# A fused attention and recurrence kernel: position biases from row and column sums on GpSimd, raw last chunks, another order at the end and a branch hint

## The chip, the cores and the metric

The kernel runs on one core of one Trainium2 chip. The metric is the device time of one execution in microseconds. Names of engines: PE is TensorE, DVE is VectorE, ACT is ScalarE, POOL is GpSimd, SP is SyncE; PEld is TensorE's weight load.

## What is computed

The input x has the shape (8, 128, 48, 48): 8 images, 128 channels, 2304 positions. Cut to what matters:

```python
# layer 0: causal attention on the group-normed image, with a position table (32 rows) appended
x0 = concat([gn(x), pe], axis=1).reshape(B, 160, N)
q, k, v = (leaky_relu(W @ x0 + b) for W, b in ((Wq, bq), (Wk, bk), (Wv, bv)))
x = x + softmax(mask(q.T @ k / sqrt(128))) @ v
# layer 1: attention of the normed tokens with themselves, then a recurrence over the positions
t = tokens(x)
n = ln(t);  t2 = t + softmax(n @ n.T) @ n
wx = ln(t2) @ W.T;  wx = (wx - mean(wx)) * rsqrt(var(wx) + 1e-5) * gamma + beta     # over all tokens
y_p = sigmoid(wx_p + y_{p-1} @ V.T)          # p = 0 .. 2303, y_{-1} = 0
out = t2 + y
```

The position table has two halves: row j < 16 depends only on the image row, row j >= 16 only on the image column. A last row of ones carries the biases. So the part of q and k that comes from the table is, for each channel, a value of the image row plus a value of the image column.

## The kernel before

`fast_path` computes everything under two assumptions (bounded logits; a recurrence that forgets its start), tests them at the end, writes `flag`, and `conv_attn_hybrid_kernel` (L1703) branches on it: at a flag of zero it jumps over `general_path`, a long program that does the work again without the assumptions.

**The attention part.** Each image's 2304 positions are cut into six chunks of 384 (`QC`), each of three blocks of 128. For image b the class `Causal` runs the first attention: for chunk j and block m a product `s` (L1038), its exponential `p` on ScalarE (L1040), on the diagonal a multiplication with a triangle on GpSimd (L1043), and a product `o` (L1049). The sums of p go to VectorE (`acc`, L1060, L1064). `Full` does the second attention in the same way (L1316, L1318, L1341), but uses each p twice: a transposed copy goes to memory (`e`) and comes back as `g` for another chunk (L1329). The tiles p come from six buffers, and products `o` follow their `s` three items later (`LAG`).

The order of instructions on each engine is written out by the program itself: `Stream` keeps chains of small steps with the costs that their author gave them, and runs a step when its time has come; a step with an empty engine name is a pure delay. `st.advance` and `st.finish` force steps of a chain to be emitted now. What the hardware then does is in order on each engine; DMAs are issued by SyncE in the order of its queue, a few by GpSimd.

**The head.** For image 0, `positions(n, j)` (L836 to L853) multiplies the position table's 33 rows with the weights of q, k (j = 0, 1: one product of 384 columns, L847) and v (j = 2: three of 128, L850), and ScalarE copies the result from PSUM into a tile `pb` (L851), which is also stored for the other images (L853). Beside it VectorE computes the group norm: six `bn_stats` (L805) as pieces of x land (`load_x`, three pieces of two chunks), an aggregate, two small products, and a power on GpSimd (L669). `project` (from L875) then norms a chunk (`xn`, L892), multiplies it with the weights (L899, L902), adds `pb` (L906), applies the leaky ReLU (L907), and takes maxima for the bound on the logits (L921).

**After a chunk of the second attention.** `Full.after` copies o out of PSUM (L1361), transposes it (L957), computes t2, its mean and variance (L1376 to L1385, L938 to L941), and the root on GpSimd (`rooted`, L1398). For most chunks t2 is then turned by a store and a load (`spread` L1412, `fetch` L1416), multiplied raw with the centred weights (`product` L1424) and only then scaled by the root, which is spread over the partitions by memory (L1409, L1418). The mean falls out because the weights are centred. The last two chunks of the last image avoid memory: t2 is transposed (`keep_last`, `turned_back`, L965), and beside it a normed copy is made (`normed`, L952), transposed (`back`), and multiplied (`statistics`, L1464), with `bn_stats` on the result (L1469). `keep` (L1438 to L1445) collects t2 in a tile `t2c` for two chunks, of which there is one buffer; `store` writes it out. Ahead of it, `keep` forces the chunk before to be finished. `idle` (L1505) issues products of the identity with itself, which fill TensorE's waits.

**The recurrence.** The 2304 positions are cut into 96 segments of 24 in three groups, which run side by side from 10 warm-up steps ahead. Before it, the statistics of all chunks are joined (L1595), and scale and shift of the batch norm are computed. VectorE writes the scaled inputs into PSUM (`inputs`, L1617, L1620), TensorE adds the product with the state (L1666), ScalarE takes the sigmoid (L1667). t2 is added by GpSimd or VectorE and stored (`add_residual`, L1643 to L1647). A product with the bounds of the logits (`pw`, L1650) goes with `fl`. After the last step VectorE adds the last residuals, compares the states at the seams of the segments (`seams`, L1635 to L1638), and TensorE adds up the result for `flag` (L1695 to L1698).

## Time and profile before

| what | us |
|---|---|
| median of three runs | 1719.08 |
| the runs | 1713.53, 1719.08, 1719.97 |
| the profiled execution | 1715.02 |
| its span | 1713.3 |
| TensorE busy | 1687.8 |
| VectorE busy | 1209.1 |
| ScalarE busy | 684.8 |
| GpSimd busy | 449.9 |
| last sigmoid ends | 1698.06 |
| `flag` written | 1704.88 |

The page of the profile gives the busy time of each engine, a view of the span in 40 slices, the chain of work that ended last, and the costliest groups of instructions. A line such as "PE MATMUL o<-p,vT 128*128 128x384" is an instruction with its program line, the tile it writes, the tiles it reads, and its size. A product of float32 values is recorded as two instructions. "idle before <-releaser" is how long the engine stood still, and what ended that. Times in a timeline count from the start of the span.

### The profile page before, as it was taken

How to read it: one execution, taken by the hardware profiler on the slowest of the kernel's cores; microseconds unless marked ns; L12 is line 12 of the kernel's file. 1: busy time of each engine (PE TensorE's matmuls, PEld its weight loads, DVE VectorE, ACT ScalarE, POOL GpSimd, SP SyncE). 2: the span in 40 equal slices, each digit the busy share in tenths (PEclk: the TensorE clock that was granted, in tenths of full speed). 3: DMA queues.
4: the chain of work that ended last, by engine and by line, in shares of the span. 5: the costliest groups of instructions: out<-in, count | busy, mean ns of one | idle time of the engine just before them, and what ended most of it. 6: DMA issues, size and time to landing. Idle time of an engine off the chain costs nothing.

```text
span 1713.3 us, 22451 instructions
## 1 busy us (share of the span) xinstructions
PE 1687.8 (99%) x6259; PEld 1085.4 (63%) x6259; DVE 1209.1 (71%) x3297; ACT 684.8 (40%) x1300; POOL 449.9 (26%) x637
## 2 busy tenths in 40 slices
PE   9999999999999999999999999999999999999986
PEld 5666666666666666666666666666666666666665
DVE  5875578666886578865787568865798657974467
ACT  3344334433344324443244333443244442443355
POOL 1233122312133122322124112331213221341205
PEclk9999999999999999999999999999999999999998
DMA  3337763568445774368735684448743686347857
GB/s 122 101 89 210 225 200 109 131 193 251 129 129 145 238 230 128 79 189 244 205 101 130 199 252 139 125 130 244 227 146 71 176 244 207 81 96 211 237 221 223
DMA packets 316731, 291.67 MB, mean 170 GB/s; under 512 B 195793, under 2 KB 280690, under 8 KB 315956
## 3 DMA queue, kind: packets, MB, share of 16 engines
q1 hardware_dynamic: 306572, 268.76, 54.7%
q0 software_dynamic: 9792, 20.99, 4.5%
q8 instruction: 52, 0.85, 0.2%
q14 instruction: 83, 0.68, 0.1%
q10 hardware_dynamic: 232, 0.40, 0.1%
HBM read 164.13 MB, written 125.90 MB: 169 GB/s over the span
## 4 chain that ended last, share of the span: by engine, by line
PE 96%; DMA 2%; DVE 1%; SPq 0%; issue 0%; ACT 0%; DVEq 0%; ACTq 0%
PE s L1038 17%; PE s L1316 17%; PE o L1049 17%; PE o L1341 17%; PE o L1329 13%; PE pj L899 3%; PE pj L902 2%; PE o L1337 2%; PE z L1666 2%; PE wx L1424 2%; DMA g<-e 1%; PE of_t L957 1%; PE pb L847 0%; PE idle_last L1505 0%; DMA x<-in_x_dram 0%; DMA e<-t 0%
## 5 line engine op out<-in xcount | busy, mean ns | idle before, releaser
L1318 ACT ACTIVATE p<-s,shift 128x384 f32<-128x384 f32 (+2 forms) x504 | 274.2, 550 | 535.9 <-PE s L1316 436.8
L1040 ACT ACTIVATE p<-s 128x384 f32<-128x384 f32 (+2 forms) x504 | 229.4, 460 | 400.1 <-PE s L1038 323.6
L1038 PE MATMUL s<-q,k 128*128 128x384 f32 (+2 forms) x1008 | 380.6, 459 | 0.1
L1316 PE MATMUL s<-xh 128*128 128x384 f32 (+2 forms) x1008 | 379.2, 458 | 0.0
L1049 PE MATMUL o<-p,vT 128*128 128x384 f32 (+2 forms) x1008 | 377.5, 456 | 0.0
L1341 PE MATMUL o<-p,xhT 128*128 128x384 f32 (+2 forms) x1008 | 369.1, 456 | 0.0
L1281 DVE STREAM_TRANSPOSE t<-p 128x384 f32<-128x384 f32 x360 | 186.0, 553 | 170.8 <-DMA e<-t 106.3
L1329 PE MATMUL o<-g,xhT 128*128 128x384 f32 x720 | 282.2, 489 | 0.7 <-DMA g<-e 0.7
L1341 PEld LDWEIGHTS o<-p,xhT 128*128 128x128 f32 x1008 | 189.7, 190 | 120.3
L1049 PEld LDWEIGHTS o<-p,vT 128*128 128x128 f32 x1008 | 186.9, 190 | 109.9 <-POOL p L1043 2.0
L1316 PEld LDWEIGHTS s<-xh 128*128 128x128 f32 x1008 | 183.2, 191 | 99.6 <-issue 0.2
L1038 PEld LDWEIGHTS s<-q,k 128*128 128x128 f32 x1008 | 183.4, 190 | 99.0 <-issue 2.2
L1064 DVE TENSOR_TENSOR acc<-acc,p 128x384 f32<-128x384 f32 (+2 forms) x408 | 212.5, 521 | 23.1 <-DVE acc L1064 1.0
L1329 PEld LDWEIGHTS o<-g,xhT 128*128 128x128 f32 x720 | 132.6, 191 | 80.2 <-DMA g<-e 2.2
L1043 POOL TENSOR_TENSOR p<-p,triu 128x128 f32<-128x128 f32 x144 | 71.3, 497 | 356.1 <-ACT p L1040 355.8
L1266 POOL DMA_DIRECT2D gm<-m x192 | 105.3, 555 | 179.1 <-PE s L1316 63.2
L1262 POOL DMA_DIRECT2D m<-tm x48 | 29.9, 623 | 374.5 <-DVE tm L1249 374.5
L1138 POOL TENSOR_SCALAR xhT<-xhT 128x384 f32<-128x384 f32 x48 | 60.5, 1260 | 150.5 <-DVE yt L1150 121.2
L1249 DVE STREAM_TRANSPOSE tm<-p 128x256 f32<-128x256 f32 x96 | 33.9, 366 | 73.1 <-ACT p L1318 72.3
L899 PE MATMUL pj<-xn,wT 128*128 128x384 f32 x192 | 77.9, 488 | 1.5 <-DVE xn L892 1.5
L947 POOL TENSOR_TENSOR rs_c<-ve_c,mhalf 128x3 f32<-128x3 f32 x48 | 48.2, 1004 | 96.1 <-DVE ve_c L941 86.8
L906 DVE TENSOR_TENSOR q<-pj,pb 128x384 f32<-128x384 f32 x48 | 26.6, 554 | 50.1 <-PE pj L899 50.1
(256 smaller groups left out, 1681.1 us busy)
## 6 DMA issues: line engine op xcount, KB each, us to landing
e<-t SPq DMA_DIRECT2D x480, 144.0 KB
g<-e SPq DMA_DIRECT2D x120, 576.0 KB
pb<-posb_d SPq DMA_DIRECT2D x42, 576.0 KB
t1t<-in_x_tok_dram SPq DMA_DIRECT2D x48, 192.0 KB
m<-tm POOLq DMA_DIRECT2D x48, 192.0 KB, 4.3
gm<-m POOLq DMA_DIRECT2D x192, 48.0 KB, 3.8
t_d<-tt SPq DMA_DIRECT2D x184, 48.0 KB
t2x<-t_d SPq DMA_DIRECT2D x46, 192.0 KB
```

The lines of the kernel that those rows point to most:

```text
L899: nc.tensor.matmul(ps[:, :QC], wT[:, j, :], xn, start=True, stop=True)
L1038: nc.tensor.matmul(s[:, off:QC], keys[b][:, ts(m, P)], queries[b, j][:, off:], start=True, stop=True)
L1040: nc.scalar.activation(p[:, off:], s[:, off:QC], AF.Exp, scale=SCALE)
L1043: nc.gpsimd.tensor_mul(p[:, off : off + P], p[:, off : off + P], triu)
L1049: nc.tensor.matmul(o[:, off:QC], vals[b][:, ts(m, P)], p[:, off:], start=first, stop=last)
L1064: nc.vector.tensor_add(a[:, off:], a[:, off:], p[:, off:])
L1266: nc.gpsimd.dma_start(gm[ts(r, SQ)].rearrange("c a q r -> c a (q r)"), d.rearrange("(a c) b f -> b c a f", a=R)[r])
L1281: nc.vector.transpose(t[:, :, :, g, :].rearrange("p b j r -> p j b r"), p.rearrange("p (j b r) -> p j b r", j=QB, b=R))
L1316: nc.tensor.matmul(s[:, off:QC], xh[:, ts(m, P)], xh[:, j * QC + off : (j + 1) * QC], start=True, stop=True)
L1318: nc.scalar.activation(p[:, off:], s[:, off:QC], AF.Exp, bias=shift)
L1329: nc.tensor.matmul(out_ap, xhT[:, QB * i + g, :], p, start=first, stop=last)
L1341: nc.tensor.matmul(o[:, off:QC], xhT[:, what[1], :], p[:, off:], start=first, stop=last)
```

## The change

- **Positions.** For chunks 1 to 5, the parts j = 0 and 1 of `pb` are no longer products. `separate(h)`, for each half of the table, multiplies the weights with one column of positions for each image row (24 columns) and, in the first half, with the 48 positions of the first row. ScalarE copies the parts, with the corner value taken off once, into space of the tile `wx` that is not yet used. GpSimd then adds a row part and a column part, each broadcast, into `pb`. Chunk 0 and the part j = 2 stay products. The first x is loaded in four pieces (2, 2, 1, 1 chunks).
- **Raw last chunks, spread roots.** The last two chunks of the last image are multiplied raw, from `t2c` (`raised`), and scaled afterwards by the root. The root is spread by three products: the root of a token, broadcast as weights, with the identity. `normed` and `back` go. The steps of chunk 4 get later due times. The table of the sigmoid is loaded by a small instruction on `scrap`; fillers on TensorE change.
- **End.** The product with the bounds moves ahead of the recurrence, in place of eight fillers. Two of the last six residual sums are made by TensorE (`summed`: identity with t2, then identity with y, into one PSUM bank, and a copy by ScalarE). The seams come ahead of the other four sums, of which three come behind `flag`.
- **Branch.** `flag` is now 1 where the fast result is kept. The taken branch still jumps over the general path, and a hint for it, "likely taken", is given on all engines.

In the built program the hint is the first instruction of each engine's stream behind its first branch. GpSimd's order in the head becomes: two sums, the power of the group norm, four sums, three triangle products, a sum, a triangle product, a sum, two triangle products, two sums. On TensorE the three transposes of chunk 4 of the last image come seven products later than before, and the spread-root products of chunk 4 stand directly ahead of the transposes of chunk 5's result.

```diff
-        load_x(0, (2, 2, 2))
+        load_x(0, (2, 2, 1, 1))
...
+            if j < 2 and n:
+                rows = by_row[:, j, ds((n - 1) * RC, RC)].unsqueeze(2).to_broadcast([P, RC, W])
+                columns = by_column[:, j, :].unsqueeze(1).to_broadcast([P, RC, W])
+                nc.gpsimd.tensor_add(made[n][:, j, :].rearrange("p (r w) -> p r w", w=W), rows, columns)
+                return
...
+        def separate(h):
+            ps = psum_t(f"pos_parts_{h}")
+            n = H // 2
+            parts = ps[:, : 2 * (n + W)].rearrange("p (j k) -> p j k", j=2)
+            for j in range(2):
+                first = pe_sb[h][: NPE + 1].rearrange("e (r w) -> e r w", w=W)[:, :, 0]
+                nc.tensor.matmul(parts[:, j, :n], wpT[: NPE + 1, j, :], first, start=True, stop=True)
+                if h == 0:
+                    nc.tensor.matmul(parts[:, j, n:], wpT[: NPE + 1, j, :], pe_sb[0][: NPE + 1, :W], start=True, stop=True)
+            if h:
+                nc.scalar.copy(by_row[:, :, n - RC :], parts[:, :, :n])
+                return
+            corner = small2.tile([P, 2], F32, tag="qk", name="pos_corner")
+            nc.scalar.activation(corner, parts[:, :, n], AF.Copy, scale=-1.0)
+            for j in range(2):
+                nc.scalar.activation(by_column[:, j, :], parts[:, j, n:], AF.Identity, bias=corner[:, j : j + 1])
+            nc.scalar.copy(by_row[:, :, : n - RC], parts[:, :, RC : n])
...
+                def raised():
+                    tp = psum_t(f"wr_{b}_{j}")
+                    k = j % (SG // SJ)
+                    nc.tensor.matmul(
+                        tp[:, :QC].rearrange("p (l s) -> p l s", l=LS), w1T, self.t2c[:, :, ts(k, SJ)], start=True, stop=True
+                    )
+                    c["wr"] = chunk_tile("scale", f"wr_{b}_{j}", c, 5, bufs=1)
+                    nc.scalar.copy(c["wr"], tp[:, :QC])
 
                 def statistics():
                     tp = psum_t(f"wx_{b}_{j}")
-                    nc.tensor.matmul(tp[:, :QC], w1T, c["xc"], start=True, stop=True)
+                    by_token = tp[:, :QC].rearrange("p (a g r) -> p g a r", a=R, g=QB)
+                    for g in range(QB):
+                        nc.tensor.matmul(by_token[:, g], c["rs"][:, g : g + 1].to_broadcast([P, P]), ident, start=True, stop=True)
+                    if final:
+                        nc.scalar.activation(scrap, half, AF.Sigmoid)
                         idle(psum_s("idle_last2"), 8)
+                    z = c["wr"].rearrange("p (l s) -> p l s", l=LS)
+                    nc.vector.tensor_mul(z, tp[:, :QC].rearrange("p (s l) -> p l s", l=LS), z)
+                    nc.vector.bn_stats(most[:, 3:] if final else stats[:, b * NQ + j, :], c["wr"])
+                    nc.scalar.copy(wx[:, :, b, ts(j, SJ)], z)
...
-                        (keep_last, 0.35, [("ACT", 0.85)]),
-                        (normed, 0.0, [("DVE", 1.1)]),
-                        (back, 0.35, [("ACT", 0.5)]),
-                        (statistics, QC * US, [("DVE", 0.55), ("ACT", 0.85)]),
+                        (keep_last, 0.35, [("ACT", 0.85), ("", 0.0 if final else 3.0)]),
+                        (raised, QC * US, [("ACT", 0.5), ("", 0.0 if final else 1.0)]),
+                        (statistics, 0.35, [("DVE", 1.1), ("ACT", 0.85)]),
...
-                    (rooted, 0.0, [("POOL", 0.9)]),
+                    (rooted, 0.0, [("POOL", 0.9), ("", 5.0 if last and not final else 0.0)]),
...
         idle(psum_s("idle"), 12)
+        separate(0)
         for j in range(3):
             positions(0, j)
+        for j in range(2):
+            positions(1, j)
         gn = st.add(group_norm(0))
-        idle(psum_s("idle_m"), 2)
         st.advance(gn, 2)
         idle(psum_s("idle_e"), 4)
         st.finish(gn)
+        idle(psum_s("idle_r"), 6)
         for j in range(2):
-            positions(1, j)
+            positions(2, j)
         project(0, 0)
         st.advance(projected[0, 0], 4)
+        separate(1)
         st.advance(projected[0, 1], 1)
         positions(1, 2)
...
-        idle(pw[:, 2 * P :], 8)
+        nc.tensor.matmul(pw[0:1, :B], ones[:, 0:1], bound, start=True, stop=True)
...
-        for l0 in range(LM, LS, TZ):
-            for g in range(G):
-                add_residual(g, l0, ys[g, l0])
+        def summed(g, l0):
+            z = ps_z[g].tile([P, TZ, B, SG], F32, tag="z", name=f"zr_{g}_{l0}")
+            for part, start in ((tokens_of(g, l0), True), (ys[g, l0], False)):
+                nc.tensor.matmul(z, ident, part, start=start, stop=not start)
+            r = rlast.tile([P, TZ, B, SG], F32, tag="r", name=f"r_{g}_{l0}")
+            nc.scalar.copy(r, z)
+            return partial(nc.sync.dma_start, out[g, :, l0 : l0 + TZ], r)
+
+        summed(0, LS - TZ)()
         for g in range(G):
             seams(g)
...
+        store = summed(1, LS - TZ)
         nc.tensor.matmul(pw[0:1, P : P + 1], off, ones[:, 0:1], start=True, stop=True)
-        nc.vector.tensor_scalar(flag, pw[0:1, P : P + 1], fl[:, 1:2], 0.5, ALU.add, ALU.is_gt)
+        for g in range(G):
+            add_residual(g, LM, ys[g, LM])
+            if g == 0:
+                store()
+                nc.vector.tensor_scalar(flag, pw[0:1, P : P + 1], fl[:, 1:2], 0.5, ALU.add, ALU.is_le)
+        add_residual(2, LS - TZ, ys[2, LS - TZ])
...
-    with tc.If(redo > 0):
+    tc.mark_branch_hint_location("redo", "LikelyTaken", engines=list(nc.engines))
+    kept = nc.values_load(flag[0:1, 0:1], min_val=0, max_val=1, skip_runtime_bounds_check_because="the flag is the result of a comparison")
+    with tc.If(kept > 0, preferred_fallthrough_block=False, label="redo") as same:
+        pass
+    with same.Else():
         general_path(tc, *args)
```

## The prediction

> **What bounds the kernel now.** I read the page first, then busy time by stretch, then the chain and timeline of the two ends.
>
> ```profile
> span 1713.3 us, 22451 instructions
> PE 1687.8 (99%) x6259; PEld 1085.4 (63%) x6259; DVE 1209.1 (71%) x3297; ACT 684.8 (40%) x1300; POOL 449.9 (26%) x637
> ...
> PE 96%; DMA 2%; DVE 1%; SPq 0%; issue 0%; ACT 0%; DVEq 0%; ACTq 0%
> ```
>
> TensorE is busy 1687.8 of 1713.3 us, so 25.5 us can be idle, and elsewhere only removed TensorE work helps.
>
> ```profile
> core 0: us, PE busy (x) PEld busy (x) DVE busy (x) ACT busy (x) POOL busy (x), PEclk, DMA share, GB/s
> 12.50:50.00 37.50, 36.84 (x145) 21.49 (x145) 23.29 (x50) 13.46 (x30) 4.33 (x9) 1.00 0.29 106
> 50.00:90.00 40.00, 39.08 (x146) 24.90 (x145) 37.89 (x106) 13.16 (x29) 11.19 (x13) 1.00 0.44 113
> 90.00:1600.00 1510.00, 1509.26 (x5495) 960.03 (x5494) 1074.58 (x2985) 598.96 (x1110) 393.68 (x548) 1.00 0.60 169
> 1600.00:1641.00 41.00, 36.71 (x130) 22.95 (x128) 16.31 (x49) 13.68 (x21) 7.37 (x12) 0.96 0.66 193
> 1705.00:1713.30 8.30, 0.00 (x0) 0.00 (x0) 0.00 (x0) 0.00 (x0) 0.00 (x0) 0.50 0.05 15
> ```
>
> From 90 to 1600 us TensorE idles 0.7 us, and there the order of instructions is unchanged: nothing is to be won or lost. Three places are open: the head (TensorE full to 50 us while VectorE idles 14.2; VectorE 95% busy from 50 to 90), the last chunks (1600 to 1654), and the end, whose last 8.3 us hold no work.
>
> **The head.** Twelve products `pb` of L847 become two; ten become GpSimd sums. In the timeline (start, duration, engine, line, out<-in; x2 because each product goes in two passes):
>
> ```profile
> 38.47 0.91 PE L1038 MATMUL s<-q,k 128*128 128x384 f32 x2
> 39.21 0.81 PE L1049 MATMUL o<-p,vT 128*128 128x384 f32 x2
> 39.95 0.91 PE L847 MATMUL pb<-pe,wpT 33*128 33x384 f32 x2
> 40.79 0.91 PE L1038 MATMUL s<-q,k 128*128 128x384 f32 x2
> 41.54 0.59 PE L1049 MATMUL o<-p,vT 128*128 128x256 f32 x2
> ```
>
> From o to the next o is 2.33 us with a `pb` between, against 2 x 0.65 = 1.30 in the steady part: a `pb` costs TensorE 1.03 us, as both neighbours lose their hidden weight load. Two of the ten lie at 10.97 us, under the group norm, and are worth nothing; eight at 18 to 40 us give 8.2 us. Ten ScalarE copies of 0.48 us go as well, hidden. Added: six products of 24 or 48 columns and five small ScalarE steps. The first four run from 6.2 us, when the table has landed, before `pb`, under the wait for x, and the other two beside a remaining 33-row product: 0.2 us. The fourth piece of x lets the last bn_stats be one (0.51 us) instead of two (1.02): 0.4 us earlier, or nothing if the smaller piece lands later (its issue comes 0.45 us later).
>
> The sums: GpSimd's four adds of 128x512 took 5.27 us at 1672, so 1.0 us for 384 columns. Queue: the two for chunk 1 stand ahead of the group norm's power, from about 7.9 to 9.9, and the power is due at 10.8; it is covered with 0.9 us to spare, and costs what the sums exceed that. Later ones stand ahead of the triangle products; behind a product of scores there are three items of 1.3 us before its p is needed, so one or two adds are covered. The positions' stores on SyncE wait for the sums, and behind them t1t loads, all early enough.
>
> How much of 8.2 survives VectorE? Its work stays. Walking the new order through with the durations above, TensorE reaches `s` of chunk 3 about 8.7 us earlier and the projection of chunk 4 some 9.8 (also a 0.9 us wait on xn at 56.2 goes), but VectorE is gapless from about 38 us and runs only 7.0 us earlier at chunk 4; six p buffers then hold TensorE back for 1 to 2 us. I take 8.5 us for the head, bounds 4.5 and 10.5.
>
> A rule that speaks against this: the Trainium skill, "SBUF — State Buffer", section "Who interferes with whom", has a VectorE instruction with two SBUF inputs and a GpSimd instruction that reads SBUF exclude each other for the whole instruction. The trace is milder: at 35.64 us an acc sum took 0.81 us instead of 0.55 beside a triangle product that took 0.64 instead of 0.45. By the row eight adds cost VectorE 2 us; by the rule up to 8, of which its idle time (14.2 less the compression of 8) hides 6: 2 us off the gain. I take the row.
>
> **The last two chunks.**
>
> ```profile
> 1623.64 2.24 DMA t_d<-tt
> 1625.96 5.39 DMA t2x<-t_d
> 1631.35 0.14 issue
> 1631.49 0.88 PE wx L1424 x2
> ```
>
> In the chain of waits (start, length, what it was), TensorE waits 4.0 us for t2x, behind the transposes of chunk 4; three products after it then take 3.31 us instead of 1.94 (the clock in this stretch is 0.96). Now the built order has seven more products ahead of these transposes. Their g tiles land (completion events) at 1628.64 and 1630.34, so they run to 1631.6 and t2x is then in. The next wait is new: `raised` reads t2c, whose copy waits for the store of the tile before (0.78 us of wait, copy at 1634.96), so the product can start at 1635.5: some 2 us idle. The last o then ends near 1637.4 instead of 1640.67, 3.3 us earlier. But the spread-root products of chunk 4 are forced behind it, and behind them on VectorE, in order: multiply 0.56, bn_stats 0.57, bn_aggr 1.43, two small ones; only then `dn` of chunk 5, at 1640.9 instead of 1641.82. **0.9 us** is left of 3.3.
>
> From `dn` on, t2 and its root come as before; removed are three normalizing steps (0.86), three transposes (0.5), a copy (0.48) and the product behind the root. In their place behind the root (ready 1645.2 in the new times): three products (0.67) and one VectorE multiply (0.56): bn_stats starts at 1646.7 instead of 1648.98, i.e. 2.3 earlier, **1.4** beyond the 0.9. The sigmoid table (1.28 us at 1651.38) is loaded under the VectorE work: 1.4. And the eight fillers `pw` (1652.23 to 1654.02) no longer hold `bound`, on which VectorE waited:
>
> ```profile
> DVE fl L1652 <- PE pw L1650: 1.2, 1, 1.2
> ```
>
> Then the inputs z_-8, the next thing late, start near 1651.1 instead of 1654.44. The recurrence moves by **3.3 us**; bounds 1.5 and 4.3.
>
> **The end**, in the times of before, relative to the last sigmoid at 1698.06.
>
> ```profile
> 1700.20 1.31 DVE L1646 TENSOR_TENSOR r<-y,t2s 128x512 f32<-128x512 f32 x2 [0.45 <-DMA out_dram<-r]
> 1701.43 0.41 DVE L1635 TENSOR_TENSOR d<-y,warm 128x248 f32<-128x248 f32 x1
> 1704.67 0.21 DVE L1698 TENSOR_SCALAR flag<-pw,fl 1x1 int32<-1x1 f32 x1 [0.28 <-PE pw L1697]
> ```
> ```profile
> L1712 PEldq COMPARE_BRANCH  x1: 3462/3462/3462, 1705.5 to 1705.5; - x1
> L1712 POOLq EVENT_SEMAPHORE  x1: 17/17/17, 1709.6 to 1709.6; - x1
> L1751 POOLq DRAIN  x3: 46/107/2685, 1709.7 to 1713.0; - x3
> ```
>
> The first fence is the timeline of the end, the second what the rows of the branch's lines hold (count, then min/median/max in ns, then first and last start). Today: flag at 1704.88, its load 0.5, the branch until 1709.0 (TensorE) to 1709.8, GpSimd's drain 2.69, closing steps 0.8. After: the seams (2.61 us) follow the loop's four sums, 1697.3 to 1699.9, `off` to 1700.24. TensorE makes the two sums first, four products of 512 columns at 0.86 us (the 384-column pair took 0.65), from 1697.7 to 1701.15; so the flag is at 1701.65 and GpSimd would be through at 1706 with a free branch. Behind the flag VectorE still makes three sums (0.62 each) to 1703.5; SyncE issues the last store at 1703.55. In before the last store went out at 1701.92 and its last piece landed at 1705.86, with the DMA full; now, with fewer ahead of it, I take 1705.9 again (bounds 1705 and 1707). SyncE then works off its remaining waits (0.062 us each, some 1.0) and the closing 0.8 follow: 1707.7, **5.5 us** less than 1713.3. The stores, not the flag, are then late last.
>
> With no use of the hint, SyncE branches at 1704.7, gets its code 3.7 us later, and ends at 1710.6: 2.7 us. Here the second rule speaks against the change: the Trainium skill, "Runtime: NRT & Kernel Launch", "Instruction fetch mechanics", calls prefetch purely sequential, and a taken branch out of a window of two pages a stall. The rows agree on the stall (3.46 us). In the built program the hints stand at the very start of each engine's stream, about 1700 us ahead of the branch; by the rule their effect is nil. No run here shows a hint. I take it that it is kept until its branch, and keep both ends.
>
> **Sum.** 8.5 + 3.3 + 5.5 = 17.3 us. The profiled execution took 1715.02 us for the span of 1713.3, so 1697.7. The three runs shown have a median of 1719.08, from 1713.53 to 1719.97, so from the median it is 1701.8. I predict **1700.0**. Less than 0.5%, 8.6 us, cannot be told from no change.
>
> **Rivals.** (A) The hint does nothing: 14.5 us gained, 1703. For it, the rule and its place; against it, that it names its branch. Chance 0.22. (B) VectorE swallows half of the head (gain 4.5, from its 95% at 50 to 90 us, and full exclusion by GpSimd): 1704. Against it, its 14.2 us of idle time before. 0.15; (A) and (B) together, 1707, 0.08. (C) The slower one: an armed hint takes the place of sequential fetches. The queue of 16 KB instruction packets has 52 of them; each late one costs up to 3.46 us, so from five late fetches on the kernel is slower, and with a quarter of them late, 45 us, it takes 1745. Against it speaks only that hints would be useless then. 0.05. The sums as predicted: 0.50, own range 1694 to 1706.
>
> Over these: faster 0.82 (all of the first case but 0.02, most of A and B, a third of A with B), same 0.11, slower 0.07 (C, and small mishaps). The range leaves out C and the worst sums: 1692 to 1711.
>
> **What would show it.** The head: `s` of chunk 3 near 44 us (now 52.5), ten GpSimd sums of about 1 us. Last chunks: no wait of 4 us on t2x, one of 2 us before `raised`, `dn` waiting for bn_aggr, the first z product 3 to 4 us earlier against the last o. The end: COMPARE_BRANCH short on all engines, under 10 us from the last sigmoid to the end (now 15.2). Wrong would be: VectorE waits that grow after 40 us, a branch still at 3.5 us, or gaps between instructions in the middle.

## The result, and the profile after

The changed kernel takes 1702.73 us (median of six runs, 1701.26 to 1704.94), the kernel before, measured beside it, 1714.15 us. The ratio is 0.992 with a 95% interval from 0.9904 to 0.9937: faster, by more than the 0.5% that counts as a difference here, and 2.7 us above the forecast of 1700.0. The profiled execution took 1704.94 us, the slowest of the six, with a span of 1703.1 us against 1713.3: 10.1 us less, where the working expected 17.3. The forecast stood on the three runs of before known then, with a median of 1719.08 us; with three more it is 1714.15. So the time came out near the forecast, but the gain, 11.4 us by the medians, is two thirds of the one that was worked out.

The page of the changed kernel, the span and the busy times:

```profile
span 1703.1 us, 22445 instructions
PE 1684.7 (99%) x6249; PEld 1086.7 (64%) x6249; DVE 1208.4 (71%) x3291; ACT 683.5 (40%) x1298; POOL 461.0 (27%) x647
```

TensorE is busy for 3.1 us less only. Ten products went, but parts, fillers and sums came, so the sum alone doesn't say where the time is. The windows of the changed kernel show where to look. The columns are busy time and instructions of each engine, then the granted TensorE clock, the DMA share and GB/s.

```profile
core 0: us, PE busy (x) PEld busy (x) DVE busy (x) ACT busy (x) POOL busy (x), PEclk, DMA share, GB/s
0.00:12.50 12.50, 10.74 (x55) 9.86 (x55) 4.02 (x10) 3.40 (x8) 6.71 (x31) 0.87 0.58 189
12.50:50.00 37.50, 36.59 (x163) 25.67 (x164) 30.82 (x66) 10.97 (x25) 12.67 (x18) 0.95 0.33 114
50.00:90.00 40.00, 40.00 (x143) 25.10 (x142) 36.84 (x103) 13.72 (x30) 12.15 (x13) 1.00 0.43 114
90.00:1600.00 1510.00, 1507.35 (x5489) 958.79 (x5488) 1070.36 (x2976) 598.41 (x1107) 394.37 (x548) 1.00 0.61 169
1600.00:1641.00 41.00, 37.91 (x167) 25.71 (x165) 18.63 (x59) 13.89 (x21) 7.37 (x12) 1.00 0.62 177
```

VectorE is busy for 30.82 us from 12.5 to 50 us instead of 23.29, so its idle time there is used, as the working wanted. But the clock is 0.87 and 0.95 in the first two stretches, where it was 1.00 before, and TensorE's idle time from 90 to 1600 us has grown from 0.7 to 2.7 us.

To follow the time I cut both traces at the same instructions: the first pass of a product of scores `s`; the pass with the number 60 of these (counted from 0, two passes to a product), which lies behind the head; the pass 1000 of the 1008 of the second attention's scores, late in the last image; the end of the last sigmoid; the end of the last instruction.

| stretch | before, us | after, us | difference | forecast |
|---|---|---|---|---|
| start to the first scores | 15.70 | 19.02 | +3.32 | about 0 |
| first scores to pass 60 | 55.05 | 46.53 | -8.52 | -8.5 |
| pass 60 to pass 1000 | 1540.89 | 1542.97 | +2.08 | 0 |
| pass 1000 to the last sigmoid | 86.42 | 82.96 | -3.46 | -3.3 |
| last sigmoid to the end | 15.19 | 11.65 | -3.54 | -5.5 |
| sum | 1713.26 | 1703.13 | -10.13 | -17.3 |

Two of the five stretches came out to within 0.2 us; three did not. Here is the start in the timeline of the changed kernel (start, duration, engine, line, out<-in).

```profile
10.33 2.05 PE L1540 MATMUL idle_e<-ident 128*128 128x128 f32 x8
...
12.18 0.43 PE L825 MATMUL gn_v<-gn_e,grp 128*128 128x1 f32 x2
12.46 2.91 PE L1540 MATMUL idle_r<-ident 128*128 128x128 f32 x12
12.64 0.16 DVE L669 TENSOR_SCALAR ve_gn<-gn_v 128x1 f32<-128x1 f32 x1 [1.52 <-PE gn_v L825]
...
13.49 0.98 DVE L923 TENSOR_SCALAR xn<-x,gn_mg,gn_rs 128x384 f32<-128x384 f32 x1 [0.69 <-POOL gn_rs L670]
...
15.16 1.95 PE L930 MATMUL pj<-xn,wT 128*128 128x384 f32 x4
...
19.02 0.91 PE L1069 MATMUL s<-q,k 128*128 128x384 f32 x2
```

The same steps in before:

```profile
9.79 1.14 PE L1505 MATMUL idle_e<-ident 128*128 128x128 f32 x8
...
11.08 0.16 DVE L668 TENSOR_SCALAR ve_gn<-gn_v 128x1 f32<-128x1 f32 x1 [0.51 <-PE gn_v L824]
...
11.94 0.48 DVE L892 TENSOR_SCALAR xn<-x,gn_mg,gn_rs 128x384 f32<-128x384 f32 x1 [0.70 <-POOL gn_rs L669]
...
15.70 0.91 PE L1038 MATMUL s<-q,k 128*128 128x384 f32 x2
```

The eight passes of `idle_e` take 2.05 us instead of 1.14, and `gn_v`, a product that the group norm needs, is queued behind them: VectorE waits 1.52 us for it (0.51 before). `xn` takes 0.98 us instead of 0.48 beside the GpSimd sums that start at 13.44, and the twelve passes of `idle_r` hold TensorE until 15.2. The windows of the clock's own stretches say why:

```profile
5.92:9.33 3.41, 3.41 (x23) 2.75 (x22) 2.46 (x5) 1.41 (x6) 0.93 (x2) 1.00 0.64 198
9.33:12.75 3.42, 3.42 (x17) 3.20 (x16) 0.65 (x4) 0.71 (x2) 0.87 (x2) 0.50 0.43 172
12.75:16.16 3.41, 3.41 (x14) 3.09 (x14) 1.03 (x2) 0.00 (x0) 2.28 (x3) 0.50 0.00 0
```

TensorE ran at half clock from 9.33 to 16.16 us, although it was busy without a gap before. In the later images the loss is at one wait (waits of TensorE from 90 to 1600 us: what waited, total, times, longest; before it was 0.7, 2, 0.6):

```profile
PE o L1360 <- DMA g<-e: 2.5, 2, 1.3
```

The last chunks and the change to the recurrence, in the timeline:

```profile
1631.90 0.91 PE L1495 MATMUL wr<-t2c,w1T 128*128 128x384 f32 x2 [2.04 <-ACT t2c L1472]
...
1636.08 1.43 DVE L1398 BATCH_NORM_AGGREGATE most<-stats 128x2 f32<-128x282 f32 x1
...
1637.68 0.55 DVE L1407 TENSOR_REDUCE dn<-of_t 128x3 f32<-128x384 f32 x1
...
1642.01 1.28 ACT L1507 ACT_TABLE_LOAD   x1
```

The 4.0 us wait on t2x is gone, and `raised` has its wait of 2 us on t2c. From pass 1000 on (3.13 us earlier than in before), the last product o gained 3.4 us (it ends at 1634.12 instead of 1640.67), but `dn`, which comes directly behind the long aggregate, only 1.0 of them (1637.68 instead of 1641.82). The table's load ends at 1643.29, before ScalarE's next copy is due at 1643.66. This is the chain as the prediction walked it.

At the end, the lines of the branch (count, min/median/max in ns, first and last start):

```profile
L1774 SPq EVENT_SEMAPHORE  x8: 17/17/17, 1698.4 to 1701.4; - x8
L1774 ACTq COMPARE_BRANCH  x1: 68/68/68, 1695.7 to 1695.7; - x1
...
L1774 PEldq COMPARE_BRANCH  x1: 5046/5046/5046, 1695.8 to 1695.8; - x1
...
L1774 ACTq EVENT_SEMAPHORE  x1: 17/17/17, 1696.2 to 1696.2; - x1
...
L1774 PEldq EVENT_SEMAPHORE  x1: 51/51/51, 1700.9 to 1700.9; - x1
```

ScalarE's next instruction comes 0.5 us after its branch, and so it is on GpSimd and SyncE; on TensorE the branch still takes 5.05 us. SyncE is through with the branch at 1698.4, but its eight waits for the last stores end at 1701.4 only; these set the end.

### The profile page after: what moved, and what is told of

Its sections match the earlier page's. It is cut to its first block, busy times and chain, and to the rows that moved or that the text cites. A ratio compares the mean times of both kernels' runs of the same rounds, so it can differ in the third digit from the quotient of the medians.

```text
span 1703.1 us, 22445 instructions
## 1 busy us (share of the span) xinstructions
PE 1684.7 (99%) x6249; PEld 1086.7 (64%) x6249; DVE 1208.4 (71%) x3291; ACT 683.5 (40%) x1298; POOL 461.0 (27%) x647
## 4 chain that ended last, share of the span: by engine, by line
PE 95%; DMA 2%; DVE 1%; SPq 0%; issue 0%; POOL 0%; ACT 0%; DVEq 0%; POOLq 0%; ACTq 0%
PE s L1347 17%; PE s L1069 17%; PE o L1372 17%; PE o L1080 17%; PE o L1360 12%; PE pj L930 4%; PE z L1714 2%; PE pj L933 2%; PE o L1368 2%; PE wx L1455 2%; DMA g<-e 1%; PE of_t L988 1%; DMA e<-t 0%; PE dn L1128 0%; PE tb L988 0%; DMA t2x<-t_d 0%
```

## The experiments

Theories. Mine: the change did what it says in the places that it touches, and the gain was given back outside of them, to a half clock and to waits for g that differ from one execution to the next, and to stores that land late. The rival: the head is worth only what its profiled execution showed (3.1 us at the end of the second attention), and the hint did little.

### One part undone at a time

The branch hint left out of the changed kernel:

```diff
-    tc.mark_branch_hint_location("redo", "LikelyTaken", engines=list(nc.engines))
```

> The changed kernel without the branch hint, all else the same. Theory 1 (the hint is kept for 1700 us and saved four engines the stall; the landing of the stores, at 1701.42 us, hides most of it): the branch takes 3.4 to 5 us on every engine again; SyncE is through at about 1701.6 instead of 1697.9, works off eight waits on stores that are long done and twelve closing ones, and the end is 0.8 us later (0.3 to 1.6). Theory 2 (the hint did nothing, and the branches are short because the taken block lies behind the general path now): branches of 0.07 us followed by the next instruction 0.4 to 0.5 us later here as well, except on TensorE, and the time of the changed kernel. Beside it: the head is that of the changed kernel. If its 6.8 us of half clock are the phase of one execution, the first product of scores starts here at some 16.5 us; if they come from the order of its products, at 19.0.

The head of before in the changed kernel:

```diff
-        load_x(0, (2, 2, 1, 1))
+        load_x(0, (2, 2, 2))
...
-            if j < 2 and n:
-                rows = by_row[:, j, ds((n - 1) * RC, RC)].unsqueeze(2).to_broadcast([P, RC, W])
...
-        separate(0)
...
+        idle(psum_s("idle_m"), 2)
```

> The changed kernel with the head of before (twelve position products on TensorE, three pieces of x, the old fillers). Theory 1 (the head is worth what its profiled execution showed at the end of the second attention, 3.1 us): 3 us slower than the changed kernel. Theory 2 (the profiled execution met a half clock by chance, which cost it some 3 us, and waits for g later, which cost 2.1): 6 to 8.5 us slower. Either way the first product of scores starts near 15.7 us and that of chunk 3 near 52.5, as in before.

The last two chunks of before in the changed kernel (with `normed`, `back` and the old `statistics`, the old delay, and the fillers ahead of `bound`):

```diff
-                        (keep_last, 0.35, [("ACT", 0.85), ("", 0.0 if final else 3.0)]),
-                        (raised, QC * US, [("ACT", 0.5), ("", 0.0 if final else 1.0)]),
-                        (statistics, 0.35, [("DVE", 1.1), ("ACT", 0.85)]),
+                        (keep_last, 0.35, [("ACT", 0.85)]),
+                        (normed, 0.0, [("DVE", 1.1)]),
+                        (back, 0.35, [("ACT", 0.5)]),
+                        (statistics, QC * US, [("DVE", 0.55), ("ACT", 0.85)]),
```

> The changed kernel with the last two chunks of before (normed copy, second transposes, table loaded late, fillers ahead of the bound). Theory (their gain is one of its own, 3.45 us by the traces): last sigmoid and end 3.4 us later, the 4 us wait of TensorE on t2x is back. Rival (part of the gain is only the head's, passed on, or a half clock after the long wait): under 2.5 us.

The order of before at the end of the changed kernel:

```diff
-        summed(0, LS - TZ)()
+        for l0 in range(LM, LS, TZ):
+            for g in range(G):
+                add_residual(g, l0, ys[g, l0])
         for g in range(G):
             seams(g)
...
```

> The changed kernel with the order of before at the end (all sums on VectorE and GpSimd, then the seams, then the flag), the hint kept. From the last sigmoid: flag at 6.8 us, its load 0.8, a short branch 0.5, GpSimd's drain 2.7, closing 0.8: 11.6 us, which is what the changed kernel took (11.62). Theory 1 (the landing of the stores is what bounds the end of the changed kernel, and the new order buys nothing beside the hint): within 0.7 us of the changed kernel. Theory 2 (the order brought the 3.6 us, the hint nothing): 3.6 us slower. If TensorE's branch takes 5 us here too, it ends 13.5 us after the last sigmoid, 1.9 us slower.

The four ran on the same chip, before beside them at 1716.0 us. Medians, ratios to before, and the stretches of the profiled executions:

| kernel | median, us | ratio (95%) | first scores | to pass 60 | to pass 1000 | to last sigmoid | to end |
|---|---|---|---|---|---|---|---|
| no hint | 1702.79 | 0.9922 (0.9908 to 0.9935) | 16.34 | 48.16 | 1540.40 | 85.30 | 12.06 |
| old head | 1709.28 | 0.9968 (0.9955 to 0.9981) | 21.32 | 55.62 | 1541.91 | 82.02 | 11.76 |
| old chunks | 1707.67 | 0.9948 (0.9936 to 0.9960) | 19.39 | 46.52 | 1542.30 | 86.54 | 11.25 |
| old end | 1702.31 | 0.9918 (0.9905 to 0.9931) | 18.33 | 46.52 | 1541.90 | 83.44 | 11.38 |

*The hint.* The branch of the kernel without it:

```profile
L1773 SPq EVENT_SEMAPHORE  x8: 17/17/17, 1699.2 to 1700.0; - x8
...
L1773 POOLq COMPARE_BRANCH  x1: 54/54/54, 1694.5 to 1694.5; - x1
L1773 PEldq COMPARE_BRANCH  x1: 4920/4920/4920, 1694.5 to 1694.5; - x1
...
L1773 SPq COMPARE_BRANCH  x1: 45/45/45, 1696.6 to 1696.6; - x1
...
L1773 POOLq EVENT_SEMAPHORE  x1: 17/17/17, 1698.3 to 1698.3; - x1
```

GpSimd goes on 3.8 us after its branch and SyncE 2.5, instead of 0.5 each. So the hint works on these engines, 1700 us after it was given, and theory 2 of this run falls; by the rule that the prediction set against it, its effect would have been nil. Yet the end is only 0.4 us later (12.06 against 11.65), and the median is that of the changed kernel (1702.79 against 1702.73). The new order does the rest: the branch runs beside the landing of the stores.

*The old end with the hint* takes 11.38 us from the last sigmoid, no more than the new one, as its theory 1 said. Here the hint worked on TensorE too:

```profile
L1761 SPq EVENT_SEMAPHORE  x8: 17/17/17, 1698.0 to 1698.5; - x8
...
L1761 PEldq COMPARE_BRANCH  x1: 392/392/392, 1697.5 to 1697.5; - x1
```

By the traces, the hint alone brings 15.19 - 11.38 = 3.8 us, the order alone 15.19 - 12.06 = 3.1, and both together 3.5: they take away nearly the same time. (TensorE's branch was short in the first of these three traces and long in the other two. With the new order and the hint, three traces with a short branch there, the old chunks and two below, ended 11.25 to 11.38 us after the last sigmoid, and three with a long one 11.65 to 11.76, so it goes with 0.3 to 0.4 us.)

*The old chunks* cost 4.9 to 5.4 us by the medians of these runs and 3.1 us against the old-end kernel by the stretch of the traces (86.54 to 83.44), with the 3.9 us wait on t2x back. The theory held. But its rival, a half clock after the long wait, isn't out: this trace has one from 1627.92 to 1631.33 us, and so have all three traces with the old last chunks (before, this one, and before with wide fillers, below: 86.42, 86.54 and 84.63 us in this stretch). Of the eleven with the new ones two have it (no hint, 85.30, and the first other end, 84.67); the other nine took 82.0 to 83.6. The other 2 us of the medians aren't explained: 1.5 of them lie ahead of pass 1000 in this pair of traces, where both kernels have the same instructions.

*The old head* costs 6.5 to 7.0 us by the medians; theory 2 of that run was nearer than theory 1. Its eleven runs lie in two groups, six from 1707.3 to 1709.3 us with a mean clock of 0.999, and five from 1711.8 to 1715.3 with 0.996 and less; against the lower one alone the head is worth 5.5 to 6.0 us. The profiled run is of the upper group, and its trace contradicts what both theories said of its start: the first scores at 21.32 us, where the same instructions gave 15.70 in before. From 10.57 to 24.22 us its clock was at half:

```profile
7.16:10.57 3.41, 3.10 (x18) 2.27 (x17) 1.88 (x5) 1.44 (x3) 0.00 (x0) 1.00 0.32 76
10.57:17.40 6.83, 6.83 (x19) 4.51 (x19) 1.28 (x6) 0.96 (x2) 0.58 (x1) 0.50 0.21 86
```

So the half clock isn't a matter of the new head alone. And the first scores of the three kernels with the new, unchanged head were at 16.34, 19.39 and 18.33 us: it isn't the same from one execution to the next either.

### What turns the clock down

In every trace the clock changes at steps of 3.41 us, counted from its first rise, which came anywhere from 4.6 to 7.9 us. I weighed each pass of a product by its rows: a pass over n columns holds the array for as long as the trace shows from one start to the next without waiting (0.112 us for 128 columns and 0.3225 for 384 at full clock, twice that at half), and counts with rows/128. For the 3.41 us from 5.92 on in the changed kernel: fillers of 128 rows for some 0.6 us, the parts and `pb` products of 33 rows for the rest, a share of 0.32, though TensorE was never idle.

| stretches of 3.41 us up to the last sigmoid, in 14 traces (before, after, the twelve experiments) | number | weighed share |
|---|---|---|
| full clock, full in the next | 6877 | 0.396 and more |
| full clock, half in the next | 18 | 0.37 and less |
| half clock, full in the next (14 of them the first rise of a trace) | 30 | 0.76 and more |
| half clock, half in the next | 15 | 0.76 and less |

Without the weights the shares of the 18 reach up to about 0.75, while the clock stayed full after stretches of some 0.45, so busy time alone doesn't separate them. The Trainium skill ("TensorE: Matmul & The Clock Gate", Part 1) has a free-running window of about 3.4 us, and that the count of slow products differs between runs; both agree with the rows here. That rows count is from these traces alone, found after the first four experiments; the next ones test it in part: they add products of 128 rows, so both shares rise. No run changed the rows alone with the busy time held, so something else that goes with the 33-row products isn't ruled out.

Before, with one edit:

```diff
+        def wide(tp, n):
+            for _ in range(n):
+                nc.tensor.matmul(tp[:, : 3 * P], ident, ident.unsqueeze(1).to_broadcast([P, 3, P]), start=True, stop=True)
...
-        idle(psum_s("idle_m"), 2)
+        wide(psum_s("idle_m"), 2)
```

> The kernel before with one edit: in place of the two 128-column fillers idle_m ahead of the group norm's product, two of 384 columns. It adds 1.29 - 0.22 us of TensorE work under a wait. Theory 1 (TensorE's clock is judged by the clock's own stretches of 3.41 us, and falls to half after one in which products, each weighed by its rows out of 128, fill under about 0.4 of it; the 33-row position products of the head are what is too little, and whether it happens depends on where the stretches lie): no half clock before 1600 us, the first product of scores near 15.7 us in any execution, the median 2 to 3 us below before, and the slow half of the times (1716 to 1719) gone. Theory 2 (the half clock comes by chance, whatever TensorE does there): the spread and the median of before, within 0.5 us.

Measured: 1713.02 us, before beside it 1714.26, ratio 0.9991 (0.9983 to 0.9999). The gain of the median is 1.2 us, less than the expected 2 to 3. The spread is the test: the 27 runs of before reach from 1710.73 to 1720.25, ten of them above 1716.0, with mean clocks of 0.991 to 0.994, the others with 0.995 and more; the 22 runs with the edit reach from 1711.80 to 1714.99, none with a clock under 0.995. The upper group is gone by adding TensorE work, so theory 2 falls; as only ten of the 27 were in it, the median gained little. Its trace has full clock through the head, and the first scores at 16.06:

```profile
4.71:8.12 3.41, 3.21 (x21) 2.51 (x21) 1.63 (x4) 0.79 (x2) 1.10 (x4) 1.00 0.92 282
8.12:11.54 3.42, 3.42 (x20) 2.51 (x20) 2.04 (x7) 0.65 (x2) 0.00 (x0) 1.00 0.46 177
```

The changed kernel with such a head:

```diff
         separate(0)
-        for j in range(3):
-            positions(0, j)
+        positions(0, 0)
         for j in range(2):
             positions(1, j)
+        positions(2, 0)
         gn = st.add(group_norm(0))
+        wide(psum_s("idle_m"), 1)
         st.advance(gn, 2)
-        idle(psum_s("idle_e"), 4)
+        positions(0, 1)
+        wide(psum_s("idle_e"), 1)
         st.finish(gn)
-        idle(psum_s("idle_r"), 6)
+        positions(0, 2)
+        wide(psum_s("idle_r"), 1)
...
```

> The changed kernel with a head that keeps TensorE at 128 rows: 384-column fillers between the 33-row products in place of idle_e and idle_r, one behind the first product of scores, k's and v's position products behind the group norm's, and the first sum of chunk 2 ahead of the group norm's root on GpSimd. Theory 1 (half clock and late position products are what made the head start 3.3 us late): full clock up to 1600 us, first product of scores at 15.7 to 16.4 us, product 60 of the scores at 64.0 to 64.6 us (70.75 in before, 65.55 in the changed kernel), median 1 to 1.5 us under the changed kernel. Theory 2 (VectorE alone sets the pace after 38 us): the start is earlier, product 60 is not (64.5 or later), and the median is that of the changed kernel.

Measured: 1702.55 us, 0.992 (0.9903 to 0.9938), no different from the changed kernel. The expectation of the clock failed: the stretch from 7.1 us had a weighed share of 0.30, so one filler was too little, the clock fell from 10.49 to 17.32 us, and the first scores came at 19.83.

The same with memsets for the sums:

```diff
-                nc.gpsimd.tensor_add(made[n][:, j, :].rearrange("p (r w) -> p r w", w=W), rows, columns)
+                nc.gpsimd.memset(made[n][:, j, :], 0.0)
```

> The kernel of the run before it, with the ten GpSimd sums replaced by memsets of the same tiles (so the position parts of q and k are left out for chunks 1 to 5): GpSimd reads nothing there and holds its queue for less. Theory 1 (the sums' contention, 2.2 us of longer VectorE instructions in the traces, sets the head back): product 60 of the scores 1.5 to 2.2 us earlier. Theory 2 (most of it falls where VectorE waits anyway): under 0.7 us.

Measured: 1701.99 us, 0.9921 (0.9899 to 0.9943). From the first scores to pass 60 it took 45.94 us against 46.58: behind the first scores 0.6 us is all that the sums cost the stream, and theory 2 holds there. Ahead of them this run says nothing, since the memsets stretched an `xn` too (1.27 us beside three of them, 0.98 beside a sum). (Pass 60 itself came 2.6 us earlier, but 2.0 of that is the half clock of its start, which was one stretch shorter.) In the trace of the changed kernel the VectorE instructions that overlap a sum took 2.2 us longer than the median of their kind, 1.16 of it on three `xn` and 0.62 on one `acc`. One of them, a `k` of 0.85 us, also lay beside a triangle product, and took as long in the run with the memsets.

### The end in other orders

The changed kernel with four sums, the seams, and then the flag:

```diff
-        summed(0, LS - TZ)()
+        first = summed(0, LS - TZ)
+        for g in range(G):
+            add_residual(g, LM, ys[g, LM])
+        first()
+        second = summed(1, LS - TZ)
+        add_residual(2, LS - TZ, ys[2, LS - TZ])
+        second()
         for g in range(G):
             seams(g)
```

> The changed kernel with its end in a third order: the four sums on VectorE first, beside the two by TensorE, then the seams and the flag; hint kept. From the last sigmoid, by the rows of the runs so far: four sums end at 1.8 us, the second sum by TensorE is copied at 3.6, so the last store goes out at 3.7; landing 4.4 later and 1.9 for SyncE's waits and the closing: 10.0. Flag at 5.2, load 0.8, branch 0.5, drain 2.7, closing 0.8: 10.0. Theory 1 (both orders are bound by what they put last): 10.0 us (9.6 to 10.6), 1.6 less than the changed kernel. Theory 2 (the stores' landing is bound by what the memory takes in, whatever the order): 11.3 or more.

Measured: 1701.54 us, 0.9917 (0.9901 to 0.9934); 12.06 us from the last sigmoid to the end. Neither theory is right: the stores had landed by 1695.1, but TensorE's branch took 4.38 us and SyncE waited 2.8 us for it. The head of this run had full clock, and shows what the new head is worth then: first scores at 16.31, pass 60 at 62.84, 7.9 us earlier than in before.

The same with TensorE's branch moved by seven fillers:

```diff
+        idle(pw[:, 2 * P :], 7)
         nc.tensor.matmul(pw[0:1, P : P + 1], off, ones[:, 0:1], start=True, stop=True)
```

> The kernel with the third order of the end, with seven fillers on TensorE ahead of the flag's product, where it waits 2.5 us for VectorE. They shift TensorE's branch from instruction 3248 of its program to 3255; the hinted branch was short at 3242, 3244 and 3260 and took 4.4 to 5 us at 3248. Theory 1 (the hint's failure on TensorE hangs on where the branch lies in its instruction stream): branch of 0.4 to 0.5 us, and the end 10.6 us after the last sigmoid, with GpSimd's drain as its bound, instead of 12.06. Theory 2 (it hangs on what TensorE did before, the sums that it makes at the end): 4.4 us again, 12.0.

Measured: 1702.11 us, 0.9922 (0.9897 to 0.9947). The two rows, the first of the kernel without the fillers:

```profile
L1774 PEldq COMPARE_BRANCH  x1: 4380/4380/4380, 1694.1 to 1694.1; - x1
```

```profile
L1775 PEldq COMPARE_BRANCH  x1: 486/486/486, 1695.4 to 1695.4; - x1
```

The end came 10.24 us after the last sigmoid, the shortest of all; theory 1 holds. That the fillers themselves did it, by what they make of TensorE just ahead of the branch, is unlikely: the two kernels with a new head above have the end of the changed kernel word for word, and their branch, shifted by the head alone, was short (0.39 us). In the hinted kernels of this case TensorE's branch was short at instruction 3242, 3243, 3244, 3255 and 3260 of its program, and long in all four traces at 3248. What it is about that place isn't known.

Both ends together, and the changed kernel once more beside it:

```diff
         separate(0)
+        wide(psum_s("idle_m"), 2)
...
+        positions(2, 0)
         gn = st.add(group_norm(0))
...
+        positions(0, 0)
+        wide(psum_s("idle_e"), 1)
         st.finish(gn)
+        positions(0, 1)
+        wide(psum_s("idle_r"), 1)
...
         nc.vector.tensor_scalar(flag, pw[0:1, P : P + 1], fl[:, 1:2], 0.5, ALU.add, ALU.is_le)
+        add_residual(2, LS - TZ, ys[2, LS - TZ])
```

> Both ends of the changed kernel mended. Head: two 384-column fillers of 128 rows right behind the parts, the three position products of chunk 0 spread behind the group norm's two small products and between the projections of q, k and v, one filler after each group norm product, one behind the first product of scores. End: three sums, the seams, the flag, and only then the fourth sum; hint kept. Theory 1 (weighed by rows, every stretch of 3.41 us of the head is filled to 0.45 or more, so the clock stays full; the end is as long as what it puts last): first product of scores at 15.9 to 16.4 us in this execution, product 60 at 62.4 to 63.0, no half clock before 1600 us; from the last sigmoid to the end 9.4 to 10.3 us; median 2 to 3 us under the changed kernel run beside it, with less spread. Theory 2 (the half clock comes whatever the head does, and the end stays near 11.4): the time of the changed kernel.

> The changed kernel once more, unchanged. If the half clock of its head and the waits for g are matters of one execution: first product of scores anywhere from 16.3 to 19.5 us, product 60 of the scores 46.5 us behind it (1.6 more if the half clock falls behind the first product), the stretch from product 60 to late in the last image 1540 to 1543 us; from the last sigmoid to the end 11.6, with TensorE's branch at 5 us again. If the profiled execution of it was typical: 19.0, 65.5, 1543.

Measured: 1701.12 us, 0.9912 (0.9893 to 0.9932), for both ends; 1703.17, 0.9923 (0.9903 to 0.9942), for the changed kernel. The clock stayed full to the last sigmoid, but the first scores came at 17.48 and pass 60 at 64.53, 1.5 us later than expected. The sum of chunk 2 that was put ahead of the root is the reason: two small steps of the group norm ran into it (0.16 and 0.22 us in before).

```profile
9.86 0.69 DVE L818 TENSOR_TENSOR gn_d<-gn_mv,gn_mg 128x1 f32<-128x1 f32 x1
10.58 0.75 DVE L820 SCALAR_TENSOR_TENSOR gn_e<-gn_d,gn_mv 128x1 f32<-128x1 f32 x1
```

The end took 12.31 us, not 9.4 to 10.3: the fourth sum's store, issued at 1693.3, was seen to land at 1697.8 only, and nothing else was left to wait for. Fifteen of its sixteen signals of completion had come by 1696.0; the packets of the last piece ran from 1696.3 on, just when a 16 KB packet of instructions that had taken 1.8 us was through. So it may have stood behind that packet on one DMA engine (the trace doesn't name the engines). The changed kernel's second trace: first scores at 18.10, 48.15 to pass 60, 1542.04, 82.03, 11.66, with half clock twice (10.25 to 13.66 and 20.49 to 23.90) and TensorE's branch at 5.1 us. The end repeats to 0.01 us; the start doesn't.

Last, both ends with these two corrections (the sum back behind the root; four sums, then the seams):

```diff
-        positions(2, 0)
         gn = st.add(group_norm(0))
...
-        for g in range(2):
+        for g in range(G):
             add_residual(g, LM, ys[g, LM])
```

> The version with both ends mended, with two corrections that its trace asks for: the first sum of chunk 2 goes back behind the group norm's root (ahead of it, it stretched two small VectorE steps of the group norm from 0.16 and 0.22 us to 0.69 and 0.75), and the end takes the third order, four sums, seams, flag, with TensorE's branch at instruction 3243, where the hint works. Theory 1: no half clock before 1600 us, first product of scores about 1 us earlier than there, at 16.5 us, product 60 at 63.5; from the last sigmoid to the end 10.2 to 10.6 us; median 2 to 3 us under that version and 4 to 5 under the changed kernel, at 0.989 to 0.991 of before. Theory 2 (these microseconds are within what one execution differs from another): the median of the version with both ends mended, 0.991 to 0.993 of before.

Measured: 1700.89 us (seven runs), 0.9915 (0.9899 to 0.9930). The expected 0.989 to 0.991 was missed, and theory 2 holds. Six of the runs lie from 1699.46 to 1702.63; the profiled one took 1709.57, with half clock from 11.88 to 28.95 us:

```profile
8.47:11.88 3.41, 2.75 (x11) 1.55 (x10) 1.57 (x6) 0.48 (x1) 1.41 (x2) 1.00 0.03 5
11.88:28.95 17.07, 17.07 (x40) 10.20 (x40) 6.76 (x12) 2.52 (x6) 4.88 (x7) 0.50 0.17 68
```

The stretch from 8.47 had a share of 0.32. Once down, the clock stays down until a stretch reaches 0.76, and the mix of 33-row and 128-row products that this head spreads over its first 25 us doesn't. Its end took 12.01 us, as the fourth sum waited 2.08 us for a store that still held its buffer (0.30 in the run with the fillers). No version was told apart from the changed kernel by the intervals; the best medians lie 1 to 2 us below it.

## Why the prediction was right and where it was not

Right: faster, 1702.7 in a range of 1692 to 1711, against 1700.0; and the places of the gain. That the time is within 2.7 us is in part luck: 11.4 us were gained, not 17.3, but the median of before that the forecast started from was 4.9 us above the later one. By its own steps:

- *The head, 8.5 us, bounds 4.5 to 10.5.* From the first scores to pass 60 it brought 8.52 us in the trace, 7.9 at pass 60 with full clock, and 6.5 to 7.0 in the medians (`s` of chunk 3, awaited near 44 us, came at 48.5, and at 45.8 with full clock). The row that was taken for GpSimd's contention (eight sums cost VectorE 2 us) was right in size: 2.2 us, for ten. The rule that the prediction quotes from the Trainium skill ("SBUF — State Buffer", "Who interferes with whom"), of two instructions that exclude each other, shows in single ones (`gn_d` 0.69 us for 0.16, `acc` 1.18 for 0.56), not in all: of fifteen VectorE instructions that overlapped a sum in the changed kernel nine were hardly longer.
- *The step that failed in the head* is the start, costed at "0.2 us" for the parts and "0.4 us earlier, or nothing" for the fourth piece of x. At full clock it is 0.6 us later (16.31 against 15.70): the 0.5 that `xn` loses beside the sums of chunk 2 makes most of it, and 0.2 more is TensorE, which was still at the late parts and a `pb` when k was ready; the group norm's root came 0.14 earlier. In the profiled execution it is 3.3 later, the half clock on top. The parts were costed by their duration alone; by the shares above, they and the removed idle_m leave too little work of 128 rows to keep the clock.
- *Nothing to be won or lost between 90 and 1600 us.* The order there is unchanged, but the time was 2.1 us longer, 1.8 of it more waits for g. The fourteen traces range from 1539.8 to 1543.0 here, for old and new heads alike: this is what one execution differs from another, and a term of zero should have had that width. Why a g lands late in one execution and not in another stays open.
- *The last chunks, 3.3 us* (0.9, 1.4, 1.4 less): 3.46, by the chain that was walked. Part of it is luck of the execution: before had a half clock behind its 4 us wait and this trace none, and by the ranges above the new order gives back 1 to 3 us where it meets one.
- *The end, 5.5 us*: 3.54. Wrong is the step "I take 1705.9 again" for the landing of the stores, with its reason, fewer stores ahead. The last one was issued 5.2 us after the last sigmoid, as worked out (5.5), but landed 9.9 us after it and not 7.8. The order did that: in the six traces with all sums ahead of the seams the last landing came 6.9 to 8.2 us after the last sigmoid, in the seven with the seams first 9.5 to 10.0. The DMA shares (the last number but one) show how, in the changed kernel first, then in before:

```profile
1693.00:1694.00 1.00, 1.00 (x4) 0.38 (x2) 0.93 (x4) 0.39 (x1) 0.00 (x0) 1.00 0.29 109
...
1700.00:1701.00 1.00, 0.00 (x0) 0.00 (x0) 0.00 (x0) 0.00 (x0) 0.00 (x0) 0.50 0.06 23
```

```profile
1703.00:1704.00 1.00, 0.00 (x0) 0.00 (x0) 0.97 (x3) 0.00 (x0) 0.00 (x0) 0.50 0.97 371
...
1705.00:1706.00 1.00, 0.00 (x0) 0.00 (x0) 0.00 (x0) 0.00 (x0) 0.00 (x0) 0.50 0.06 23
```

While the seams run on VectorE, no store goes out from 1690.8 to 1693.4, and the DMA runs short: from 1693 on the share is 0.29, 0.72 and 0.76, where before kept 0.92 or more up to 1704. An estimate from these shares: 1.2 us of transfers (0.71 + 0.28 + 0.24) were put off, of the 2.1 by which the landing came later. The rest is the tail, in which one engine of 16 works (0.06), in before too; there the DMA was not full, as the prediction read it. What makes that tail longer wasn't isolated. Rival (A), the hint does nothing, gives nearly the measured time but isn't the reason: the hint works on the engines other than TensorE, and without it the end is only 0.4 us later.

Rivals (B) and (C) didn't come about: VectorE took up its part of the head, and no gaps between instructions appeared in the middle (C's late fetches): of TensorE's 2.7 us of idle time there, 2.5 are waits for g and 0.2 a wait for a triangle product.

## What to carry to other kernels

Two edits that take away the same wait are worth little more than one of them: cost each alone, and both, against the next thing late (here the landing of the last stores). Fillers that keep TensorE's clock had to be counted here in rows and columns over 3.4 us, at every place where narrow products stand together; 33-row products kept TensorE busy and still let the clock fall. An order that held back the last stores for the seams left the DMA partly idle (share 0.29 in one microsecond), and they landed later by that. Before a profile of one execution is explained, look at its clock in the first 30 us: the kernel with a weak start had times in two groups, and a microsecond of fillers took the upper one away.

## What the runs showed of the hardware beyond the expected

- TensorE's clock fell to half after every 3.41 us stretch with a row-weighed share of products of 0.37 or less (18 times) and after none with 0.396 or more (6877 times); it came back only after 0.76 or more.
- A hint given in the first microsecond was still worth 2 to 3.4 us on a branch 1700 us later on ScalarE, GpSimd and SyncE. On TensorE its effect hung on where the branch lies in its program: 0.4 to 0.5 us at five places, 4.4 to 5.1 at a sixth.
- A GpSimd sum of 128x384 with two broadcast inputs took 0.83 us, and 0.94 to 1.14 where it met an `xn`, `k` or `acc` of VectorE.
- A store of 256 KB is done by sixteen signals of completion. In one trace fifteen had come by 2.7 us after its issue, the last at 4.5.
